# Context keys in four narrow pieces for two units, a fourth key buffer, and attention values one chunk at a time

## The chip, the cores and the metric

The kernel runs on one core of one Trainium2 chip. The metric is the device time of one execution in microseconds (us), lower is better. The kernel before takes 3268.74 us, the median of three runs (3264.41 to 3271.3). The core's engines are named as the profile names them: PE is TensorE's matrix multiply, PEld its weight load, DVE is VectorE, ACT is ScalarE, POOL is GpSimd, SP is SyncE, which here does nothing but issue DMAs. A "record" is one matmul instruction in the trace; a matmul on plain float32 operands leaves two, one on float32r operands leaves one.

## The reference

Two transformer layers over x of shape (4, 512, 320), with a context of shape (4, 1601, 192). All data are float32.

```python
def _attn(x, ctx, wq, wk, wv, wo, bo, heads):          # 20 heads of 16
    q = (x @ wq)...; k = (ctx @ wk)...; v = (ctx @ wv)...
    sim = jnp.einsum('bhid,bhjd->bhij', q, k) * scale
    a = jax.nn.softmax(sim, axis=-1)
    out = jnp.einsum('bhij,bhjd->bhid', a, v)
    return out @ wo + bo

for each of two layers:
    h1 = _ln(x, n1_g, n1_b)
    x = _attn(h1, h1, q1, k1, v1, o1_w, o1_b, 20) + x      # 512 keys
    h2 = _ln(x, n2_g, n2_b)
    x = _attn(h2, context, q2, k2, v2, o2_w, o2_b, 20) + x # 1601 keys
    h3 = _ln(x, n3_g, n3_b)
    a, g = jnp.split(h3 @ ff_w1 + ff_b1, 2, axis=-1)       # 1280 wide each
    x = (a * gelu(g)) @ ff_w2 + ff_b2 + x
```

## The kernel before

**Units.** Attention is cut into units: one batch element and four of the 20 heads. A layer has 20 self units (four batches of five groups `g`), then 20 cross units, then four feed-forward units, one per batch. `u.m` counts a unit within its kind and layer. A unit's keys come in chunks of 128: 4 in a self unit, 13 in a cross unit (the last has 65 keys). All 512 queries of the batch run beside one another as the moving columns.

**A unit's main loop** (`main`, L1098). A chunk is two rounds of two heads. For each head, two float32r matmuls give the scores (L1113: keys are held as a rounded high part and a low rest, and queries too), a third subtracts the row maximum (L1116, two rows of `units` by the row `m`), and ACT writes the exponential (L1126) to one of several places. These places are the tiles of `own` and some idle weight space (`places`, `place`). Beside each round's scores goes one piece of the next unit's row maxima: two heads, 128 queries and 512 keys (L926), reduced by DVE (L947). A self unit needs 8 such pieces, a cross unit 26. Exact maxima are so found one unit ahead, and `max_end` sends them by DMA to the row tile `m` (L1006).

After a chunk's scores come the values of earlier chunks (`values`, L1133, matmul L1141): the exponentials of a chunk are the moving operand and the value columns the weights. In a self unit one chunk at a time; in a cross unit two chunks at a time, added up in one PSUM bank. ACT copies the result (L1157) and POOL adds it to the unit's output `o` (L1158).

**Banks.** `ps_st` has four PSUM banks, taken in turn by score tiles, value tiles and projections; `ps_m` has two double banks, for maxima and for the middle two quarters of context keys and values.

**Projections.** A self unit's keys (`keys`, L749) and a unit's queries (`queries`, L717) are one bank each, or two for cross queries. A cross unit's keys (`keys_of_context`, L771): the context stands transposed in four quarters of 32 rows (`QT` = 384 keys each). For six blocks of 32 input features, four quarters and two halves of a quarter there is one matmul, 48 in all, of 32x64 weights by 224 keys (`HALF + 32`; L779). Two ACT copies and one DVE copy empty the banks into `kstage`, POOL splits high and low part (`split`, L624 and L625), and six DMAs (L796, L798) bring them to the key buffer, as rows of the unit's four heads. There are three key buffers `kbuf` in turn, four query buffers in turn, and a fifth query buffer for the first cross unit of a layer. That unit (`early`) is projected up to eight units ahead.

**What sets the order.** Everything beside the main loop waits in queues (`chains`), each entry with a cost, a due round and two conditions. A round counts half a chunk. After each chunk, `steps` runs the entries with the earliest due round, as far as a credit goes that `pace` earns from costs and due rounds. DMAs out of a staging tile go to the queue `slots`, at the earliest two rounds after their producer and at most four in a chunk (L391). `slots_soon` sets `kwhen` or `qwhen` after the last of them; a unit's maxima count as at hand three rounds later (`at_hand`). The function `giver` deals out the pieces of maxima: one a round, and more, in extra groups of two pieces, where a unit would otherwise not be done in time. If nothing is at hand and the next unit is near, `at_once` runs the projection and its DMAs on the spot.

**Values** of the keys (`add_values`): three blocks of four chunks and the tail of 65 keys, each for heads 0 to 7 (`i` = 0) and 8 to 19 (`i` = 1). L869 is the matmul of a block: 24 of 32x128 weights by 128 or 192 columns.

**Feed-forward** (`ff_main`): `gate` (L1267) keeps gelu outputs in three places of `own`.

## Time and profile before

| | |
|---|---|
| median of three runs | 3268.74 us (3264.41 to 3271.3) |
| profiled execution, own time | 3267.39 us |
| its span | 3265.6 us |
| mean granted PE clock | 0.967 |
| PE busy | 3117.7 us, 95% |
| DVE, ACT, POOL busy | 64%, 57%, 30% |

| stretch of the span, us | what runs | PE busy, us | granted clock |
|---|---|---|---|
| 0 to 452 | start, 20 self units of layer 0 | 396.2 | 0.91 |
| 452 to 1305 | most of its cross units | 828.1 | 0.98 |
| 1375 to 1625 | most of its feed-forward | 249.1 | 1.00 |
| 1690 to 2083 | self units of layer 1 | 355.9 | 0.87 to 1.00 |
| 2083 to 2950 | most of its cross units | 849.2 | 0.98 |
| 2950 to 3266 | the last unit, feed-forward | 311.0 | 1.00 |

The span runs from the first to the last instruction; the device time is 1.8 us more. A group line of the profile reads: line, engine, operation, written tile <- read tile with shape, count; then busy time and mean duration; then the engine's idle time just ahead and who ended most of it. A wait line reads: engine, line, awaited engine and line, us in total, times, the longest. A timeline line reads: start, duration, engine, line, operation, count, and in brackets the idle time ahead of it. The granted clock is 1 at full speed; the record of it shows only 1.0 and 0.5 in any moment, so 0.967 means 6.6% of the span at half clock. Durations of PE are modelled at their ends, so the times that count for it are those from start to start.

### The profile page before, as it was taken

To read this page: it belongs to the slowest core of one execution; us is meant where nothing else is said; L and a number is where in the kernel's file an instruction comes from. 1 tells how busy PE (TensorE), PEld (TensorE's weight loads), DVE (VectorE), ACT (ScalarE), POOL (GpSimd) and SP (SyncE) were. 2 spreads that over 40 slices of the span, in tenths; PEclk is the share of its full clock that TensorE was granted. 3 is DMA by queue.
4 is the path that set the end of the run, shared out by engine and by line. 5 is a ranking of instruction groups with operands and counts; after the bars stand their busy time and mean duration, and the time that the engine had idled before them with its cause. 6 is when DMAs were issued, how large, how long until landed. Compare 5 with 4: busy or idle time off the path is not lost.

```text
span 3265.6 us, 89144 instructions
## 1 busy us (share of the span) xinstructions
PE 3117.7 (95%) x36690; PEld 1686.7 (52%) x36690; DVE 2077.9 (64%) x2833; ACT 1866.6 (57%) x3721; POOL 972.6 (30%) x1141
## 2 busy tenths in 40 slices
PE   7899899999999999999998998999999999999999
PEld 3455455555455555455444554555555555554555
DVE  6766777777777776522246777777777777774221
ACT  3666566776667676711126665667767777765110
POOL 2435232323323332111114453324233333322000
PEclk8999899999999999999989998999999999999999
DMA  3433222211212211200113332212112111112000
GB/s 92 91 65 77 44 43 45 54 39 38 65 33 42 60 35 28 80 4 6 27 23 73 72 62 44 41 40 51 33 39 55 36 41 39 39 22 65 9 10 15
DMA packets 213039, 145.08 MB, mean 44 GB/s; under 512 B 65556, under 2 KB 203160, under 8 KB 212632
## 3 DMA queue, kind: packets, MB, share of 16 engines
q1 hardware_dynamic: 211368, 138.32, 19.1%
q8 instruction: 289, 4.73, 0.6%
q10 hardware_dynamic: 1264, 1.06, 0.1%
q14 instruction: 118, 0.97, 0.1%
HBM read 33.04 MB, written 7.93 MB: 13 GB/s over the span
## 4 chain that ended last, share of the span: by engine, by line
PE 80%; DVE 8%; ACT 4%; issue 3%; DMA 2%; SPq 2%; POOL 1%; ACTq 0%; DVEq 0%; POOLq 0%
PE av L1141 19%; PE st L1113 19%; PE fps L1246 9%; PE st L1116 6%; PE yps L1302 5%; PE sps L926 5%; DVE pm L947 3%; PE kps L779 3%; PE qps L717 3%; PE vps L869 3%; PE ops L1050 3%; DVE nmax L947 2%; PE fps L1259 2%; ACT pr L1126 2%; PE kps L749 1%
## 5 line engine op out<-in xcount | busy, mean ns | idle before, releaser
L947 DVE TENSOR_REDUCE pm<-sps 128x2 f32<-128x1024 f32 (+1 forms) x980 | 1127.6, 1195 | 225.3 <-PE sps L926 199.6
L1113 PE MATMUL st<-q,kT 32*128 32x512 f32 (+1 forms) x5440 | 1089.3, 445 | 40.5 <-DVE x L1057 8.0
L1126 ACT ACTIVATE pr<-st 128x512 f32<-128x512 f32 (+1 forms) x1791 | 947.1, 602 | 269.9 <-PE st L1116 252.1
L926 PE MATMUL sps<-kT,q 32*128 32x512 f32 (+1 forms) x6400 | 993.6, 411 | 52.9 <-DMA kT<-stage 20.1
L1113 PEld LDWEIGHTS st<-q,kT 32*128 32x128 f32 (+1 forms) x5440 | 537.6, 182 | 482.3 <-ACT pr L1126 160.2
L1116 PE MATMUL st<-m,units 2*128 2x512 f32 (+1 forms) x2720 | 655.3, 400 | 5.9 <-issue 2.1
L1141 PE MATMUL av<-pr,vals 128*32 128x512 f32 (+1 forms) x3582 | 644.5, 636 | 16.9 <-ACT pr L1126 10.3
L1158 POOL TENSOR_TENSOR o<-o,pr 128x512 f32<-128x512 f32 x236 | 302.2, 1281 | 951.2 <-ACT pr L1157 931.2
L926 PEld LDWEIGHTS sps<-kT,q 32*128 32x128 f32 x6400 | 474.1, 188 | 103.6 <-DVE pm L947 33.3
L947 DVE TENSOR_REDUCE nmax<-sps 128x2 f32<-128x1024 f32 (+1 forms) x356 | 381.2, 1109 | 175.2 <-PE sps L926 121.6
L1126 ACT ACTIVATE wself<-st 128x512 f32<-128x512 f32 (+1 forms) x801 | 427.6, 602 | 75.1 <-PE st L1116 68.6
L1116 PEld LDWEIGHTS st<-m,units 2*128 2x128 f32 (+1 forms) x2720 | 350.7, 184 | 42.8 <-issue 7.7
L1141 PE MATMUL av<-wself,vals 128*32 128x512 f32 (+1 forms) x1602 | 344.5, 635 | 3.6 <-ACT pr L1126 3.0
L1246 PE MATMUL fps<-hT,w 128*128 128x512 f32 x640 | 285.4, 599 | 1.8 <-DVE pr L1272 0.9
L1269 ACT ACTIVATE pr<-fps,b 128x512 f32<-128x512 f32 x80 | 50.6, 683 | 370.4 <-PE fps L1259 268.1
L1141 PEld LDWEIGHTS av<-pr,vals 128*32 128x32 f32 (+1 forms) x3582 | 114.3, 112 | 236.9 <-issue 101.4
L1158 POOL TENSOR_TENSOR o<-o,wself 128x512 f32<-128x512 f32 x89 | 114.0, 1281 | 381.5 <-ACT wself L1157 381.5
L1157 ACT COPY pr<-av 128x512 f32<-128x512 f32 x236 | 140.9, 597 | 135.7 <-PE av L1141 134.7
L1246 PEld LDWEIGHTS fps<-hT,w 128*128 128x128 f32 x640 | 118.9, 190 | 151.8 <-issue 146.6
L624 POOL TENSOR_SCALAR stage<-stage 128x256 fp32r<-128x256 f32 (+1 forms) x155 | 107.1, 691 | 218.6 <-ACT stage L725 135.5
L624 POOL TENSOR_SCALAR w<-w 128x896 fp32r<-128x896 f32 x40 | 98.1, 2452 | 147.0 <-DVE w L789 118.5
L1050 PE MATMUL ops<-wo,aT 112*32 112x160 f32 (+1 forms) x3072 | 128.5, 303 | 4.1 <-ACT pr L1126 2.8
(100 smaller groups left out, 3020.8 us busy)
## 6 DMA issues: line engine op xcount, KB each, us to landing
kT<-w SPq DMA_DIRECT2D x160, 192.0 KB
q<-stage SPq DMA_DIRECT2D x320, 64.0 KB
q<-stage SPq DMA_DIRECT2D x154, 128.0 KB
aT<-o SPq DMA_DIRECT2D x320, 32.0 KB
m<-turned SPq DMA_DIRECT2D x636, 2.0 KB
kT<-stage SPq DMA_DIRECT2D x156, 64.0 KB
w<-in_L_xattn_ff_w_dram SPq DMA_DIRECT2D x20, 256.0 KB
ctxT<-ctxT SPq DMA_DIRECT2D x24, 208.0 KB
```

The costliest lines, as they stand in the source:

```text
L624: eng.tensor_scalar(high.bitcast(F32R), x, 1.0, None, ALU.mult)
L926: nc.tensor.matmul(out, lhsT=u.q[rows, e, queries].bitcast(F32R), rhs=u.kT[rows, keys].bitcast(F32R), start=(e == 0), stop=(e == 1),)
L947: nc.vector.tensor_reduce(to[:, j : j + n], part, AX.X, ALU.max, negate=(ns == 1))
L1050: nc.tensor.matmul(ps[f : f + m, : D // 2], lhsT=aT[:n, k, t * P + f : t * P + f + m], rhs=wo[:n, k, cols], start=(k == 0), stop=(k == 2),)
L1113: nc.tensor.matmul(st[:r, :], lhsT=keys, rhs=u.q[rows, e, :].bitcast(F32R), start=(e == 0), stop=False)
L1116: nc.tensor.matmul(st[:r, :], lhsT=units_of[two_rows, :r].bitcast(F32R), rhs=u.mrow[two_rows, :].bitcast(F32R), start=False, stop=True,)
L1126: nc.scalar.activation(p[:r], st[:r], AF.Exp)
L1141: nc.tensor.matmul(ps[j * SLOT : (j + 1) * SLOT, :], lhsT=columns_of[:r, head : head + SLOT], rhs=pr.pop((c, j))[:r, :], start=(c == cs[0] ...
L1157: nc.scalar.copy(vo, ps)
L1158: nc.gpsimd.tensor_tensor(u.o, u.o, vo, ALU.add)
L1246: nc.tensor.matmul(ps, lhsT=w1[:, k, i * FF + c * P : i * FF + (c + 1) * P], rhs=u.hT[:, k, :], start=ahead and k == 0, stop=not ahead and ...
L1302: nc.tensor.matmul(ps[:, :D], lhsT=hid[c][:, t * P : (t + 1) * P], rhs=w2[:, c, :], start=(c == 0), stop=(c == NHC - 1),)
```

## The change

**Context keys in pieces.** `HALF` goes and `PIECE` = 104 comes. Two neighbouring units of one batch (g = 0 and 1, or 2 and 3) are projected together: weights of 128 columns for both units, four pieces of 104 keys of each quarter, 24 matmuls a piece. The units with g = 4, and the first two cross units of a layer, are still projected alone, in two pieces of 48 matmuls with 64 weight columns. Each piece has its own entry in the queue, cost 1.1 instead of 2.45, `apart` rounds from the next. `kstage` becomes two pairs of narrower tiles, so that a piece can be staged while the last one's DMAs wait. DMAs rise from 12 to 20 for a pair and from 6 to 10 for a unit alone.

**Buffers.** `kbuf` has four tiles instead of three. The fifth query buffer goes, and the first cross unit takes its turn among the four; its queries wait until the unit four places before is scored, and are due two units ahead. `own` has seven places instead of eight, and `gate` two of them for gelu outputs instead of three.

**Due rounds.** A self unit's projections are due ten rounds ahead of the unit before, not six. The context is due earlier by the pieces' distance. The second part of the values (`i` = 1) is due 12 rounds and more sooner.

**Values.** `values(c)` takes one chunk, in cross units too.

**`giver`.** Whether to run a projection on the spot is decided by the start of the unit whose maxima are missing, not by that of the next unit.

```diff
-HALF = QT // 2
+PIECE = (QT + 32) // 4
...
-    kbuf = [const.tile([P, 4 * QT + P], F32, name=f"kT{i}") for i in range(3)]
-    qbuf = [const.tile([P, 2, N], F32, name=f"q{i}") for i in range(5)]
+    kbuf = [const.tile([P, 4 * QT + P], F32, name=f"kT{i}") for i in range(4)]
+    qbuf = [const.tile([P, 2, N], F32, name=f"q{i}") for i in range(4)]
...
-    kw = 4 * (HALF + 32)
-    kstage = [w2_flat[:, 3 * D + i * kw : 3 * D + (i + 1) * kw].rearrange("p (a w) -> p a w", a=4) for i in range(2)]
-
-    own = const.tile([P, 8, N], F32, name="pr")
-    mine = [own[:, i, :] for i in range(8)]
+    kw = 4 * PIECE
+    kstage = [
+        [w2_flat[:, 3 * D + i * kw : 3 * D + (i + 1) * kw].rearrange("p (a w) -> p a w", a=4) for i in (j, j + 1)]
+        for j in (0, 2)
+    ]
+    own = const.tile([P, 7, N], F32, name="pr")
+    mine = [own[:, i, :] for i in range(7)]
...
         if u.cross:
-            u.kT, u.k0 = kbuf[(u.m + 1) % 3], 0
-            u.other = attn[i - 3] if u.m > 1 else attn[i - 6] if u.m else None
+            u.kT, u.k0 = kbuf[(1, 2, 0, 3)[u.m % 4]], 0
+            u.other = attn[i - (6 if u.m == 1 else 3 if u.m == 2 else 4)] if u.m else None
...
             u.other = attn[i - 3] if u.m == B * G - 1 else attn[i - 4] if u.m > 3 or u.m == 3 and u.l else None
-        u.qbuf = qbuf[4 if u.early else i % 4]
+        u.qbuf = qbuf[i % 4]
...
     def stages(kind="stage"):
-        empty(kind, kind == "stage")
+        empty(kind, 1)
         if kind == "kstage":
-            return [*kstage, None]
+            kstage.reverse()
+            return kstage[0]
...
-        due = lead(u) - 6
-        keys_due = due - 10 if u.cross else due
+        due = lead(u) - (6 if u.cross else 10)
+
+        keys_due, apart = (
+            (units[u.i - 4].start, 8) if u.early else (lead(u) - 5, 3) if u.m == 1 else (due - 10, 4)
+        ) if u.cross else (due, 0)
...
             if u.cross and not u.early:
-                add_context(u.l, u.b, lambda s: u.own.update(kv=s["cT"], tail=s["tail"]), keys_due - 2, free)
+                add_context(u.l, u.b, lambda s: u.own.update(kv=s["cT"], tail=s["tail"]), keys_due - 3 * apart - 2, free)
...
-        def keys_of_context():
+        mates = [v for v in units[u.i : u.i + 2] if v.cross and v.b == u.b]
+        alone = u.m < 2 or u.g == G - 1
+        mates = [u] if alone else mates if u.g % 2 == 0 else []
+        pieces = (
+            [[(u, h * 2 * PIECE + i * PIECE, h * GD) for h in range(2)] for i in range(2)]
+            if alone else [[(v, i * PIECE, e * GD) for e, v in enumerate(mates)] for i in range(4)]
+        )
+
+        def keys_of_context(i):
...
                     rows = slice(a * SLOT, (a + 1) * SLOT)
-                    for i in range(2):
-                        w = HALF + 32
+                    for v, at, to in pieces[i] if alone else pieces[i][:1]:
+                        n = GD if alone else 2 * GD
                         nc.tensor.matmul(
-                            ps[i * GD : (i + 1) * GD, :w],
-                            lhsT=wk_q[rows, k, u.g * GD : (u.g + 1) * GD],
-                            rhs=first.kvT[rows, k, i * HALF : i * HALF + w],
+                            ps[to : to + n, :PIECE],
+                            lhsT=wk_q[rows, k, u.g * GD : u.g * GD + n],
+                            rhs=first.kvT[rows, k, at : at + PIECE],
...
                         )
-            high, low, _ = stages("kstage")
-            for i, ps in enumerate(singles):
-                nc.scalar.copy(low[:, 3 * i, :], ps[:, : HALF + 32])
-            nc.vector.tensor_copy(low[:, 1:3, :], both[:, :, : HALF + 32])
+            high, low = stages("kstage")
+            for e, ps in enumerate(singles):
+                nc.scalar.copy(low[:, 3 * e, :], ps[:, :PIECE])
+            nc.vector.tensor_copy(low[:, 1:3, :], both[:, :, :PIECE])
             split(low, high)
-            def move(e, i):
-                to = rows_of(u.kT, e)
-                if i < 2:
-                    full = to[:, : 4 * QT].rearrange("d (a w) -> d a w", a=4)
-                    dma(out=full[:, :, i * HALF : (i + 1) * HALF], in_=(high, low)[e][i * GD : (i + 1) * GD, :, :HALF])
+            def move(e, v, at, where, tail):
+                to = rows_of(v.kT, e)
+                part = (high, low)[e][where : where + GD]
+                if tail:
+                    dma(out=to[:, 4 * QT :].rearrange("d (a w) -> d a w", a=4), in_=part[:, :, QT - at :])
                     return
-                dma(out=to[:, 4 * QT :].rearrange("d (a w) -> d a w", a=4), in_=(high, low)[e][GD:, :, HALF:])
-                if e:
-                    first.made["k"] += 1
-
-            slots_soon(u, [lambda e=e, i=i: move(e, i) for e in range(2) for i in range(3)], "kwhen", "kstage")
-            u.keyed = True
-            first.made["kv"] += 1
+                full = to[:, : 4 * QT].rearrange("d (a w) -> d a w", a=4)
+                w = min(PIECE, QT - at)
+                dma(out=full[:, :, at : at + w], in_=part[:, :, :w])
+
+            fs = [
+                lambda e=e, piece=piece, tail=tail: move(e, *piece, tail)
+                for piece in pieces[i] for e in range(2) for tail in range(1 + (piece[1] + PIECE > QT))
+            ]
+            last = i + 1 == len(pieces)
+            if last:
+                fs.append(lambda: first.made.update(kv=first.made["kv"] + len(mates)))
+                for v in mates:
+                    v.keyed = True
+            slots_soon(mates, fs, "kwhen" if last else "kpart", "kstage")
         def unread():
-            return u.n < 4 or u.early or attn[u.n - 4].early or attn[u.n - 4].scored == attn[u.n - 4].nch
+            return u.n < 4 or attn[u.n - 4].scored == attn[u.n - 4].nch
         def free():
-            return u.other is None or u.other.scored == u.other.nch
+            return all(v.other is None or v.other.scored == v.other.nch for v in mates or [u])
...
             for part in range(parts):
-                add(chain, (0.05 + 0.427 / parts,) * 3, lambda part=part: queries(part), due - 2, unread)
+                add(chain, (0.05 + 0.427 / parts,) * 3, lambda part=part: queries(part), units[u.i - 2].start if u.early else due - 2, unread)
...
         else:
-            add(chain, 2.45, keys_of_context, keys_due, free)
+            for i in range(len(pieces) if mates else 0):
+                after = (3 - i) * apart if len(pieces) == 4 else (1 - i) * 2 * apart
+                add(chain, 1.1, lambda i=i: keys_of_context(i), keys_due - after, free)
...
                     "values", 0.2 + w / 100, lambda i=i, s=s: values_of_context(i, s),
-                    units[u.i + g].start + 8 * s, lambda s=s, free=free: free(4 * s + 3),
+                    units[u.i + g].start + (4 * s - 12 if i else 8 * s), lambda s=s, free=free: free(4 * s + 3),
...
         last = nxt is None or nxt.kind == "ff"
-        def values(cs):
+        def values(c):
             if u.g in (0, 2):
-                until(lambda: units[u.i - u.g].vmade[u.g // 2] > cs[-1], "values")
+                until(lambda: units[u.i - u.g].vmade[u.g // 2] > c, "values")
             ps = ps_st.tile([P, N], F32, tag="st", name="av")
-            for c in cs:
-                r = min(P, u.nkeys - c * P)
-                for j in range(HG):
-                    head = (c * H + u.g * HG + j) * VW
-                    nc.tensor.matmul(
-                        ps[j * SLOT : (j + 1) * SLOT, :],
-                        lhsT=columns_of[:r, head : head + SLOT],
-                        rhs=pr.pop((c, j))[:r, :],
-                        start=(c == cs[0]),
-                        stop=(c == cs[-1]),
-                    )
-            u.valued = cs[-1] + 1
-
-            if cs[0] == 0:
+            r = min(P, u.nkeys - c * P)
+            for j in range(HG):
+                head = (c * H + u.g * HG + j) * VW
+                nc.tensor.matmul(
+                    ps[j * SLOT : (j + 1) * SLOT, :],
+                    lhsT=columns_of[:r, head : head + SLOT],
+                    rhs=pr.pop((c, j))[:r, :],
+                    start=True,
+                    stop=True,
+                )
+            u.valued = c + 1
+
+            if c == 0:
...
                 add_finish(u)
-        n = 2 if u.cross else 1
-        together = {min(c + n, u.nch) - 1: list(range(c, min(c + n, u.nch))) for c in range(0, u.nch, n)}
...
             flush()
-            if c in together:
-                late.append(lambda cs=together[c]: values(cs))
+            late.append(lambda c=c: values(c))
...
         def gate(c, pss):
-            gl = mine[5 + c % 3]
+            gl = mine[5 + c % 2]
...
                 hand = [v for v in ahead if left(v) and all(v.pairs) and at_hand(v)]
-                if not hand and ahead[0].start - 4 - clock["round"] > 1:
+                v = hand[0] if hand else next(v for v in ahead if left(v))
+                if not hand and v.start - 4 - clock["round"] > 1:
                     break
-                v = hand[0] if hand else next(v for v in ahead if left(v))
```

Each piece, projection and DMA group is entered for both units of a pair (`slots_soon` takes a list of units), and the context is held two rounds ahead of the first piece.

More of the change, by code (lines that the diff above doesn't have):

```diff
@@ L115 @@
     nc.gpsimd.memset(units_of, 1.0)
-    fill = qbuf[4][:, 0, :]
+    fill = qbuf[3][:, 0, :]
     nc.vector.memset(fill, 1.0)
@@ L640, in stages, with slots_soon @@
     def stages(kind="stage"):
-        empty(kind, kind == "stage")
+        empty(kind, 1)
         if kind == "kstage":
-            return [*kstage, None]
+            kstage.reverse()
+            return kstage[0]
         t = two.tile([P, 2, N // 2], F32, tag="stage", name="stage")
         return [t[:, e] for e in range(2)] + [t]
-    def slots_soon(u, fs, name, kind="stage"):
+    def slots_soon(us, fs, name, kind="stage"):
         fs = list(fs)
@@ L653, in last @@
             done()
-            setattr(u, name, -9 if start["on"] else clock["round"])
+            for u in us:
+                setattr(u, name, -9 if start["on"] else clock["round"])
         group = deque(fs + [last])
         groups[kind].append(group)
-        u.slots.append(group)
+        for u in us:
+            u.slots.append(group)
         if start["on"]:
@@ L704, in add_proj @@
             if u.cross:
-                add(chain, 0.0, hold_context, keys_due - 2, yes, lambda: "kv" in u.own)
+                add(chain, 0.0, hold_context, keys_due - 3 * apart - 2, yes, lambda: "kv" in u.own)
             else:
@@ L735, in queries @@
             slots_soon(
-                u, [lambda s=s, i=i: move(s, i) for i in range(2) for s in range(2)],
+                [u], [lambda s=s, i=i: move(s, i) for i in range(2) for s in range(2)],
                 "qwhen" if part == parts - 1 else "qpart",
@@ L765, in move @@
                 )
-            slots_soon(u, [lambda e=e, i=i: move(e, i) for e in range(2) for i in range(2)], "kwhen")
+            slots_soon([u], [lambda e=e, i=i: move(e, i) for e in range(2) for i in range(2)], "kwhen")
             u.keyed = True
             first.made["k"] += 1
-        def keys_of_context():
+        mates = [v for v in units[u.i : u.i + 2] if v.cross and v.b == u.b]
[6 more added lines that the diff above has]
+        def keys_of_context(i):
             pss, singles, both = quarter_banks("kps")
```

## The prediction

> **What bounds the kernel now.** I read the page's busy line and chain first, to see which engine sets the end; then the stages, to see where that engine loses time; then the timeline inside one context unit, to see what the changed lines do there. All rows are of the one profiled execution of the kernel before.
>
> ```profile
> PE 3117.7 (95%) x36690; PEld 1686.7 (52%) x36690; DVE 2077.9 (64%) x2833; ACT 1866.6 (57%) x3721; POOL 972.6 (30%) x1141
> PE 80%; DVE 8%; ACT 4%; issue 3%; DMA 2%; SPq 2%; POOL 1%; ACTq 0%; DVEq 0%; POOLq 0%
> L1158 POOL TENSOR_TENSOR o<-o,pr 128x512 f32<-128x512 f32 x236 | 302.2, 1281 | 951.2 <-ACT pr L1157 931.2
> L624 POOL TENSOR_SCALAR w<-w 128x896 fp32r<-128x896 f32 x40 | 98.1, 2452 | 147.0 <-DVE w L789 118.5
> ```
>
> TensorE is the bound: 95% busy and 80% of the chain. A step counts here if it changes TensorE's work, its waits or its clock; GpSimd at 30% has room. By stage (stretch in us, then its length, busy time and count of PE, PEld, DVE, ACT, POOL, granted clock, DMA share, GB/s):
>
> ```profile
> 452.00:1305.00 853.00, 828.10 (x11542) 462.69 (x11541) 631.55 (x774) 595.48 (x1199) 272.77 (x267) 0.98 0.20 44
> 1690.00:1790.00 100.00, 86.36 (x968) 41.94 (x962) 63.14 (x90) 60.25 (x121) 38.51 (x41) 0.90 0.34 73
> 1790.00:1975.00 185.00, 174.65 (x2598) 97.83 (x2598) 138.54 (x209) 119.45 (x245) 91.64 (x122) 1.00 0.30 64
> 1975.00:2083.00 108.00, 94.86 (x1234) 51.24 (x1234) 81.78 (x113) 57.64 (x118) 32.49 (x31) 0.87 0.21 42
> 2083.00:2950.00 867.00, 849.21 (x11854) 473.35 (x11855) 652.42 (x766) 620.07 (x1244) 279.46 (x272) 0.98 0.18 39
> ```
>
> The two cross stages (first and last line) take over half the time with TensorE 97% busy. The starts and ends of the self stages (second and fourth) lose more per us, to idle time and to a granted clock of 0.90 and 0.87. Busy hides slow work, so the timeline of two chunks in the middle of a cross unit, in which no other work falls until the values:
>
> ```profile
> 650.41 0.50 PE L1113 MATMUL st<-q,kT 32*128 32x512 f32 x2
> ...
> 652.12 0.18 PEld L1113 LDWEIGHTS st<-q,kT 32*128 32x128 f32 x1 [0.46 <-ACT wself L1126]
> ...
> 652.44 3.12 ACT L1126 ACTIVATE pr<-st 128x512 f32<-128x512 f32 x6
> ...
> 654.16 0.39 PE L1116 MATMUL st<-m,units 2*128 2x512 f32 x1
> ...
> 656.34 0.50 PE L1113 MATMUL st<-q,kT 32*128 32x512 f32 x2
> ```
>
> The first chunk takes 1.71 us (650.41 to 652.12), less than its four exponentials (4 x 0.52, from 3.12 us for six). So in the second chunk TensorE waits for a bank before nearly every score (652.12 on): 2.36 us of scores. The values of two chunks then take 2.18 us (654.16 to 656.34). The pair: 5.93 us. Where values follow every chunk, as already in self units and in the last chunk of a cross unit:
>
> ```profile
> 448.71 0.48 PE L1113 MATMUL st<-q,kT 32*128 32x512 f32 x2
> ...
> 450.38 0.62 PE L1141 MATMUL av<-w1r,vals 128*32 128x512 f32 x1
> ...
> 451.38 0.49 PE L1113 MATMUL st<-q,kT 32*128 32x512 f32 x2
> ```
>
> Here one chunk with its values takes 2.67 us; the median of 32 such bare chunks of self units is 2.73.
>
> **The change part by part.**
>
> **Values one chunk at a time: -50 us.** Each cross unit has 13 value groups instead of 7, so 240 more in 40 units. By work alone that loses: two single groups make a pair of chunks 2 x 2.73 = 5.46 us; a pair with no ACT wait is 1.71 + 3.59 = 5.30; +0.16 x 240 = +38 us. But pairs don't run at 5.30. Of 219 pairs in the two cross stages (452 to 1290, 2083 to 2945), the 89 at full clock whose first chunk has no side work take 5.89 us on average; 113 with side work there take 5.65 once that work is taken off at its price beside single values (query part 0.66, projection 0.82: both use the value matmuls' 128-row, 32-column tiles, and now always find one beside them). 17 more ran partly at half clock. So the gain at 2.73 a chunk is (89 + 17) x 0.43 + 113 x 0.19 = 67 us. I keep 50, since 0.035 us of new wait in each of 480 chunks is easily lost: ACT then has five passes of 0.52 us = 2.6 in 2.73. Bounds: -67, and +38 if every removed wait comes back. I lean to the gain because the 23 bare single-value chunks inside the cross stages also average 2.73. The 240 more copies (0.59 us, ACT) and adds (240 x 1.28 = 307 us, POOL) are hidden: POOL goes to some 39%. If POOL were late, banks would not be (the copy frees them), only the split of keys and the end of a unit.
>
> The Trainium skill, TensorEngine Tiling (Array Packing), Key Properties, speaks against this part: changing the tiling mode drains the array. The trace agrees that it costs: 0.32 us from the last score's start to the first value matmul's, 0.53 from the last value matmul's to the next score's. By that rule alone this part is the +38 us.
>
> **Half clock in cross: -22 us.** The clock record has 17 stretches at half clock there, 68 us in all, so at most 34 us lost. Every pair that they touch, 17, has a bare first chunk, so is one of those that wait for ACT; the self stretch with single values from 1790 to 1975 has none. Bounds: -39 (the 17 pairs take 8.16 us: 17 x 2.27 over their 5.89), and +15 if the extra switches leave the array as idle. I take a little over half.
>
> **Context keys: +12 us.** L779 runs 96 records (each matmul is two) in 12 groups of eight tiles, a group every 0.19 to 0.21 us for 224 columns; with its switches a unit costs TensorE 2.75 to 2.89 us. A pair of units now takes four pieces of 48 records of 32x128 weights by 104 columns. The nearest row is L869: 48 such records add 1.65 us at 128 columns and 2.09 at 192, so 1.49 at 104 on their line, 1.65 if the weight loads set it. Per pair 5.9 to 6.6 against 5.7: +3 to +13 us for 14 pairs. The 12 units done alone run two pieces of 96 records: the group's step falls to about 0.094 us, so 12 x 0.094 + 0.55 = 1.68 each, 3.35 against 2.85: +6. If these were bound per record as now (2.85 each), +34. Below: -5, if narrow pieces lose their switches beside values. I take +12. Two ACT copies and a DVE copy per piece (about 0.25 and 0.37 us by the rows of 128 and 256 columns) and the split (two passes of 1.1 us at most instead of 2.45 and 2.11) lie beside TensorE. DMAs on SP rise from 12 to 20 for a pair and 6 to 10 alone, 160 x 0.6 us = 96 us over the span, beside other work; DMA is 20% busy. SP stands for POOL's split of a unit's keys 342 us in 40 waits, 8.6 each, and behind it stand the next unit's row maxima and queries; a split of half the length shortens each wait, and there are twice as many.
>
> The Trainium skill, TensorE: Matmul & The Clock Gate, section on 56 against 53.3 ns, has a floor of some 25 ns between starts; by it the 192 records alone cost 4.8 us and the change +38 us. The trace's eight starts of one L779 group lie within 50 ns, so I go by the group's step.
>
> **Self keys due 4 rounds sooner, no forced projection while a unit is far off: -12 us.**
>
> ```profile
> PE sps L926 <- DMA kT<-stage: 20.1, 9, 5.7
> ```
>
> These nine waits are maxima whose keys were projected and moved at the last moment; all fall in the first half of self stages, before half-clock stretches. I take 12 of the 20 and nothing for the clock. Bounds: 0 (the first units cannot start earlier, and norms gate each batch) and -40 with the clock. The moved block is 24 records, an ACT copy, two POOL passes and four DMAs, now ahead of its unit's queries on POOL and SP, which have over four rounds to spare.
>
> **First cross unit of a layer: 0.** It loses its own query buffer: its queries now wait for the fourth unit before to be scored, so its 26 maxima fall in about 14 rounds instead of some 40. Before, they already come as 14 and 11 extra groups late in the self stage, with 42 and 30 us over the single-chunk price (stretches 290 to 452, 1975 to 2083). After, about 13 extra groups of 2.6 us of DVE (0.68 x 2 + 1.22) come in a burst: 24 to 43 us. Even; bounds -25 and +45 for both layers.
>
> **Fourth key buffer, values due sooner, seven places, two gelu buffers: 0.** Three buffers let a unit's keys start when the unit two before begins; four let a pair's start just then. The later values move 12 rounds and more ahead (48 records, two ACT copies and a DVE copy a block, no DMA); their work is the same, and weight loads wait 1.9 us in all behind a values copy. FF's ACT and DVE run far below TensorE (99.6% busy there). Bounds 0 and +60: see the second rival.
>
> Sum: -50 - 22 + 12 - 12 = -72. The profiled execution took 3267.4 us, 1.8 over its span, 1.3 under the median of the three times: 3195.
>
> **The rivals.**
> *ACT paces the single chunks.* For it: 2.6 of 2.73 us of ACT and any key or query copy on top; four banks now serve five tiles a chunk. Against: the single-value chunks already seen. Then values cost +38 and the clock stays: 3267 + 38 + 12 - 12 = 3305. It decides from 2.9 us a bare chunk: 480 x 0.15 = 72 us takes the whole gain. This one ends slower.
> *Keys late at a change of batch.* A pair's four pieces need the next batch's context, which waits for the tail values of the batch before (due as before, 24 rounds into its third unit), and SP is given four queued DMAs a chunk, 20 for a pair. If half of 26 maxima come as extra groups, six changes x 6.5 groups x 3 us (the half-clock price above) = 117: 3312. Against: about 20 rounds are there for it.
> *The burst at the first cross unit costs its upper bound*, 45 us: 3240.
> *Narrow pieces change nothing and all half-clock loss goes too*: 3267 - 67 - 39 - 20 = 3141.
>
> **How the numbers follow.** My forecast 0.44 (own range 3165 to 3230), ACT 0.22, late keys 0.11, burst 0.13, all gains 0.10. The ACT case reaches from 3245 to 3305, so a few parts of it are no change. From 3140 to 3300 some 2 in 10 are left out. 0.2% is 6.5 us, about what this measurement can tell from no change. Faster: 0.44 + 0.10 + 0.11 of burst + 0.02 of ACT = 0.67; same 0.06; slower 0.27.
>
> **What would show it.** Bare cross chunks at 2.7 us with no ACT wait before a score; a granted clock of 0.99 or more in cross; key pieces at 1.5 to 1.7 us; the wait for kT below 10 us; POOL near 39%. Wrong if bare chunks take 2.9 or more, if extra groups of maxima appear at batch changes, or if the end of the self stages falls under a clock of 0.85.

## The result: 52 us less, and where it came from

The changed kernel takes **3214.66 us** (median of 4, 3211.83 to 3218.06) against 3266.57 (3262.43 to 3271.3) for the kernel before in the same comparison: ratio **0.9841, 95% interval 0.9823 to 0.9859**. The profiled execution took 3214.11, its span is 3212.3. The forecast was 3195, so the direction held and 20 of 72 us are missing.

The page of the changed kernel: busy line, chain by engine, GpSimd's adds, and the row of the score matmuls with the idle time before them at its end.

```profile
PE 3036.1 (95%) x37842; PEld 1644.5 (51%) x37842; DVE 2093.8 (65%) x2869; ACT 1963.7 (61%) x4029; POOL 1267.8 (39%) x1449
PE 77%; DVE 6%; ACT 6%; SPq 4%; DMA 3%; issue 2%; POOL 1%; ACTq 0%; POOLq 0%; DVEq 0%
L1144 PE MATMUL st<-q,kT 32*128 32x512 f32 (+1 forms) x5440 | 1001.0, 443 | 44.5 <-ACT w L810 26.8
L1188 POOL TENSOR_TENSOR o<-o,pr 128x512 f32<-128x512 f32 x359 | 461.2, 1285 | 750.4 <-ACT pr L1187 728.1
```

TensorE has 82 us less of busy time although it runs 1152 more instructions. GpSimd went from 30% to 39%, as forecast, and its adds still wait for ACT (728 us), not ACT for them. One row is new: scores that wait 26.8 us behind line 810, the ACT copy of projected context keys into their stage. It carries the rest of this text.

For the comparison I cut both spans at the same events: the moments when the row maxima of given units are finished. Rows by stage (stretch in us, length, then busy and count of PE, PEld, DVE, ACT and POOL, granted clock, DMA share, GB/s). Before: middle of the first self stage (units 5 to 15), then the two cross stages up to their last unit.

```profile
130.80:333.90 203.10, 184.98 (x2621) 102.70 (x2618) 141.60 (x231) 121.94 (x252) 90.33 (x121) 0.96 0.34 75
495.60:1339.10 843.50, 820.23 (x11169) 453.44 (x11166) 627.10 (x766) 592.25 (x1189) 265.69 (x261) 0.97 0.19 43
2124.80:2947.90 823.10, 806.76 (x11168) 448.17 (x11168) 619.46 (x721) 591.64 (x1187) 266.66 (x261) 0.98 0.18 39
```

After, the same three:

```profile
130.20:312.80 182.60, 169.98 (x2663) 95.92 (x2667) 139.22 (x228) 121.06 (x251) 92.52 (x125) 0.97 0.36 80
476.80:1313.60 836.80, 794.41 (x11466) 435.97 (x11463) 637.68 (x775) 638.38 (x1327) 401.07 (x399) 0.96 0.19 42
2082.70:2894.90 812.20, 779.22 (x11460) 430.83 (x11457) 623.90 (x734) 637.25 (x1324) 400.85 (x399) 0.98 0.18 39
```

In cross, TensorE's busy time fell by 26 and 28 us, but the stages got only 7 and 11 us shorter, and the clock did not rise. The whole sum, with the experiments' profiled spans beside it (us; in brackets the time at half clock in the cross stages):

| stretch | before | after | values singly, alone | self rounds, alone | third stage pair |
|---|---|---|---|---|---|
| self, start to unit 15, both layers | 617.5 | 585.8 | 616.2 | 599.6 | 593.6 |
| units 15 to 21, into cross | 321.9 | 326.9 | 314.6 | 314.0 | 321.5 |
| cross with its last unit | 1749.9 (82) | 1724.3 (92) | 1711.0 (68) | 1752.0 (82) | 1680.5 (37) |
| FF, both layers | 576.4 | 575.3 | 578.0 | 573.5 | 575.3 |
| span | 3265.6 | 3212.3 | 3219.8 | 3239.0 | 3171.0 |

So 32 us came from the self stages (forecast 12), 26 from cross (forecast 60), 5 were lost between them (forecast 0).

A bare chunk of a cross unit after the change, from one first score (620.46) to the next (623.17):

```profile
620.46 0.50 PE L1144 MATMUL st<-q,kT 32*128 32x512 f32 x2
...
621.52 2.07 ACT L1157 ACTIVATE wself<-st 128x512 f32<-128x512 f32 x4 [0.66 <-PE st L1147]
...
622.18 1.06 PE L1171 MATMUL av<-pr,vals 128*32 128x512 f32 x8 [0.29 <-ACT wself L1157]
...
623.17 0.44 PE L1144 MATMUL st<-q,kT 32*65 32x512 f32 x2
```

It takes 2.71 us (the median of such chunks is 2.72); the four exponentials (2.07 us) now stand idle 0.66 us before the scores are there. No score matmul shows a wait; only the values wait 0.29 us for the last exponential. That is the forecast mechanism. TensorE's longest waits over the whole span (us in total, times, longest) are others:

```profile
PE av L1171 <- ACT pr L1157: 40.7, 170, 0.3
PE st L1144 <- ACT w L810: 26.8, 15, 3.0
PE st L1147 <- DMA m<-turned: 23.3, 19, 4.1
...
PE sps L957 <- DMA kT<-stage: 8.4, 5, 3.9
```

The wait for self keys fell from 20.1 to 8.4 us. The second and third row are new (the row maxima `m` cost 1.7 us before). What is behind the second shows at a change of batch; ACT, PE, and the DMA queue of SP, each line with its idle time and what ended it in brackets:

```profile
579.73 6.16 SPq L822 DMA_DIRECT2D kT<-w  x8
...
581.61 2.94 PE L801 MATMUL kps<-ctxT,w 32*128 32x104 f32 x96
...
584.98 0.61 ACT L810 COPY w<-kps 128x104 f32<-128x104 f32 x2 [2.47 <-DMA kT<-w]
...
585.28 0.86 PE L1144 MATMUL st<-q,kT 32*128 32x512 f32 x2 [0.72 <-ACT w L810]
...
587.11 2.26 SPq L822 DMA_DIRECT2D kT<-w  x3
587.93 0.39 ACT L810 COPY w<-kps 128x104 f32<-128x104 f32 x2 [2.35 <-DMA kT<-w]
...
588.23 0.94 PE L1144 MATMUL st<-q,kT 32*128 32x512 f32 x2 [1.61 <-ACT w L810]
```

Here all four pieces of a pair are overdue, because they waited for the new batch's context, and two go into one chunk (96 records at 581.61). There are two pairs of stage tiles, so the third and the fourth piece must wait until the DMAs of the first and second have left them. SP sends these eight DMAs in 6.16 us, 0.77 each. The copy into the stage stands in ACT's queue until then (2.47 and 2.35 us), the chunk's exponentials stand behind it, and TensorE finds no free bank for scores: the keys' results hold theirs until the copy has read them.

### The profile page after: what moved, and what is told of

Read it like the earlier page. It is cut to its first block, busy times and chain, and to the rows that moved or that the text cites. A ratio compares the mean times of both kernels' runs of the same rounds, so it can differ in the third digit from the quotient of the medians.

```text
span 3212.3 us, 92658 instructions
## 1 busy us (share of the span) xinstructions
PE 3036.1 (95%) x37842; PEld 1644.5 (51%) x37842; DVE 2093.8 (65%) x2869; ACT 1963.7 (61%) x4029; POOL 1267.8 (39%) x1449
## 4 chain that ended last, share of the span: by engine, by line
PE 77%; DVE 6%; ACT 6%; SPq 4%; DMA 3%; issue 2%; POOL 1%; ACTq 0%; POOLq 0%; DVEq 0%
PE av L1171 19%; PE st L1144 16%; PE fps L1271 9%; PE st L1147 6%; PE yps L1327 5%; PE sps L957 4%; ACT pr L1157 3%; PE ops L1081 3%; PE qps L726 3%; PE kps L801 3%; PE vps L900 3%; DVE pm L978 2%; SPq L1037 2%; PE fps L1284 2%; DVE nmax L978 2%
## 5 line engine op out<-in xcount | busy, mean ns | idle before, releaser
L1157 ACT ACTIVATE pr<-st 128x512 f32<-128x512 f32 (+1 forms) x1710 | 906.7, 602 | 259.7 <-PE st L1147 250.6
L1144 PE MATMUL st<-q,kT 32*128 32x512 f32 (+1 forms) x5440 | 1001.0, 443 | 44.5 <-ACT w L810 26.8
L957 PE MATMUL sps<-kT,q 32*128 32x512 f32 (+1 forms) x6400 | 989.2, 410 | 31.2 <-DVE pm L978 11.3
L1188 POOL TENSOR_TENSOR o<-o,pr 128x512 f32<-128x512 f32 x359 | 461.2, 1285 | 750.4 <-ACT pr L1187 728.1
L1144 PEld LDWEIGHTS st<-q,kT 32*128 32x128 f32 (+1 forms) x5440 | 504.6, 184 | 471.3 <-ACT pr L1157 149.7
L1147 PE MATMUL st<-m,units 2*128 2x512 f32 (+1 forms) x2720 | 614.2, 402 | 24.4 <-DMA m<-turned 23.3
L1157 ACT ACTIVATE wself<-st 128x512 f32<-128x512 f32 (+1 forms) x867 | 462.9, 603 | 103.2 <-PE st L1147 101.6
L1188 POOL TENSOR_TENSOR o<-o,wself 128x512 f32<-128x512 f32 x191 | 245.2, 1284 | 342.1 <-ACT wself L1187 339.9
L1147 PEld LDWEIGHTS st<-m,units 2*128 2x128 f32 (+1 forms) x2720 | 313.4, 185 | 70.8 <-issue 30.9
L1187 ACT COPY pr<-av 128x512 f32<-128x512 f32 x359 | 217.1, 605 | 25.8 <-PE av L1171 24.2
L801 PEld LDWEIGHTS kps<-ctxT,w 32*128 32x128 f32 (+1 forms) x4992 | 115.4, 164 | 53.8 <-ACT pr L1157 28.7
```

Source lines behind the costliest of these rows:

```text
L801: nc.tensor.matmul(ps[to : to + n, :PIECE], lhsT=wk_q[rows, k, u.g * GD : u.g * GD + n], rhs=first.kvT[rows, k, at : at + PIECE], start=(k ...
L957: nc.tensor.matmul(out, lhsT=u.q[rows, e, queries].bitcast(F32R), rhs=u.kT[rows, keys].bitcast(F32R), start=(e == 0), stop=(e == 1),)
L1144: nc.tensor.matmul(st[:r, :], lhsT=keys, rhs=u.q[rows, e, :].bitcast(F32R), start=(e == 0), stop=False)
L1147: nc.tensor.matmul(st[:r, :], lhsT=units_of[two_rows, :r].bitcast(F32R), rhs=u.mrow[two_rows, :].bitcast(F32R), start=False, stop=True,)
L1157: nc.scalar.activation(p[:r], st[:r], AF.Exp)
L1187: nc.scalar.copy(vo, ps)
```

## The experiments

The theory after the first comparison: the values and the self rounds each bring a gain by themselves, and the reuse of the two stage pairs gives part of it back in cross, by the wait and by the half clock that follows it. Each run has a kernel before measured beside it (medians 3271.25 to 3274.32 us), and its ratio is to that. The rivals: the parts were worth less than forecast in the first place; the narrow pieces themselves are what costs (more records, more copies, more DMAs); or the late maxima rows are.

**1. Values one chunk at a time, in the kernel before.**

```diff
-        n = 2 if u.cross else 1
+        n = 1
```

> The kernel before with one thing of the change: values one chunk at a time in cross units. My theory (waits for ACT in pairs of chunks were what the cross stages lost, and key pieces and late row maxima gave back a part of it in the changed kernel): about 3210 us, cross stages 45 to 60 us shorter together, bare cross chunks at 2.8 us, less than 35 us at half clock in cross. Rival (the split values are worth little, the gain came from the self stages): 3245 us or more. Rival (the extra switches of the array cost their work): 3290 to 3305 us.

Measured: 3225.4 us, ratio 0.987 (0.9845 to 0.9895), span 3219.8: **43 us less** by the ratio, 46 by the span, 39 of them in cross. That is between my 3210 and the rival's 3245. The ACT rival is out. The two cross stages with their last units still take 1711 us, and the half clock only went from 82 to 68 us: the pairs that waited for ACT are gone here, and the slow stretches are not. So the reason I had given for the half clock fell with this run. The first cross stage:

```profile
493.80:1320.40 826.60, 791.23 (x11182) 427.05 (x11182) 635.27 (x766) 634.94 (x1298) 403.32 (x369) 0.98 0.20 44
```

It is 10 us shorter than the changed kernel's (836.80), which has the same values and less than 300 records more; the second is 3 us shorter (809.50 against 812.20). Whatever else the change did in cross, it cost.

**2. Self projections due ten rounds ahead, in the kernel before.**

```diff
-        due = lead(u) - 6
+        due = lead(u) - (6 if u.cross else 10)
```

> The kernel before with one thing of the change: self projections due ten rounds ahead instead of six. My theory now (the units' maxima are then at hand when their rounds begin, so the extra groups of maxima and the half clock after them go from the self stages): 3235 to 3245 us, all of it in the self stages. As forecast at first, for the waits on keys alone: 3255 us. Rival (it was the rule on running projections on the spot): 3267 us.

Measured: 3242.86, ratio 0.9917 (0.9901 to 0.9933): **27 us less**. That is the range I had given. Nearly all of it lies in units 5 to 15 of the first layer and in the step into cross:

```profile
133.90:316.50 182.60, 167.82 (x2546) 93.75 (x2540) 142.20 (x229) 120.85 (x250) 93.45 (x125) 0.99 0.37 81
```

That is 20.5 us less than before's 203.10, and TensorE is busy 17 us less: before, 7 groups of maxima in this stretch stood in an extra place of their own instead of beside a chunk, because their keys were not there; now one does. The clock went from 0.96 to 0.99. In the second layer the groups fall from 5.5 to 1 too, but the stretch keeps its length (195.2 against 194.1), since 20 us of it instead of 7 run at half clock.

**3. The `giver` rule, in the kernel before.**

```diff
-                if not hand and ahead[0].start - 4 - clock["round"] > 1:
-                    break
                 v = hand[0] if hand else next(v for v in ahead if left(v))
+                if not hand and v.start - 4 - clock["round"] > 1:
+                    break
```

> The kernel before with one thing of the change: whether a projection is run on the spot is decided by the start of the unit whose maxima are missing. My theory: 3260 to 3267 us. Rival (this rule gave the self stages' gain): 3240 us.

Measured: 3281.26 (3262.47 to 3284.75, 10 executions), ratio 1.0031 (1.002 to 1.0042). Nothing gained, 0.3% lost if anything, where I had expected 3260 to 3267; its profiled execution has a span of 3260.7, so a single profile would have said the opposite. The gain in the self stages is the earlier round's.

**4. These three together, in the kernel before.** (The three edits above.)

> The kernel before with single-chunk values, earlier self projections and the rule on running projections together, and none of the pieces, the shared query buffer or the fourth key buffer. My theory (the gains add, and the key pieces are a small loss): 3175 to 3190 us, faster than the changed kernel. Rival (the pieces and the fourth buffer bring some of the changed kernel's gain): 3220 us or more.

Measured: 3199.03, ratio 0.9787 (0.9766 to 0.9808), span 3198.8, 70 us less. The gains add (43 + 27), the time is 9 us above my range, and this kernel is **faster than the changed one by half a per cent**. The rest of the change, keys in pieces and buffers, costs some 15 us as it stands.

**5. The earlier self round taken out of the changed kernel.**

```diff
-        due = lead(u) - (6 if u.cross else 10)
+        due = lead(u) - 6
```

> The changed kernel with self projections due six rounds ahead again. My theory (the earlier due round alone makes the self stages' gain): 3235 to 3245 us, extra groups of maxima back in the self stages. Rival (the later projection of the first cross unit makes it too): 3220 us or less.

Measured: 3241.37, ratio 0.9896 (0.9875 to 0.9917), span 25 us over the changed kernel's. The stretch from unit 5 to 15 goes back to:

```profile
134.60:339.90 205.30, 182.58 (x2694) 101.30 (x2694) 142.20 (x228) 122.76 (x253) 93.98 (x127) 0.94 0.33 74
```

and 4.5 extra groups come back in each layer. Taken out here, the part is worth 25 us by the spans and 18 by the ratios, against 27 put in alone.

**6. Whole-unit keys in the changed kernel.** Projection, stage, DMAs and due rounds of the context keys as before; four key buffers, four query buffers, seven places and all other rounds as changed. Of the edit, the entry in the queue:

```diff
...
-            for i in range(len(pieces) if mates else 0):
-                after = (3 - i) * apart if len(pieces) == 4 else (1 - i) * 2 * apart
-                add(chain, 1.1, lambda i=i: keys_of_context(i), keys_due - after, free)
+            add(chain, 2.45, keys_of_context, keys_due, free)
...
```

> The changed kernel with context keys of a whole unit at once, as before (48 matmuls of 224 columns, one stage, their old due round), but its four key and four query buffers, seven places and all due rounds of self keys and values. My theory (the pieces cost about 15 us, the rest of the buffers nothing): 3197 to 3204 us. Rival (the loss against the three parts alone comes from the shared query buffer and the late first cross unit): 3212 us or more.

Measured: 3192.35 (3184.03 to 3194.22), ratio 0.975 (0.9732 to 0.9768), span 3182.2. **The pieces cost 30 us** as the change has them (span 3212.3), twice what I had expected. Against run 4 the span is 17 us shorter (12 by the ratios, whose intervals just touch), which is what the fourth key buffer, the later values' rounds, the seven places, the two gelu buffers and the early queries bring together; they were not tried one by one. The cross stages:

```profile
471.60:1295.00 823.40, 783.31 (x11182) 421.16 (x11186) 640.80 (x764) 635.14 (x1298) 403.86 (x369) 0.98 0.20 44
2058.80:2864.80 806.00, 776.12 (x11176) 418.06 (x11176) 627.86 (x720) 634.36 (x1295) 403.40 (x369) 0.99 0.18 40
```

This run alone does not say whether the narrow matmuls cost or their stage.

**7. The pieces kept at least four rounds apart,** so that two never fall into one chunk.

```diff
-                add(chain, 1.1, lambda i=i: keys_of_context(i), keys_due - after, free)
+                add(chain, 1.1, lambda i=i: keys_of_context(i), keys_due - after, free, lambda: clock["round"] >= clock.get("piece", -9) + 4)
```

(`clock["piece"]` is set to the current round at the start of each piece.)

> The changed kernel, but a piece of context keys is entered at the earliest four rounds (two chunks) after the last one, so that its stage has been sent off. My theory (27 us of score waits behind key copies, which stand behind the DMA out of a reused stage, and the half clock after them): those waits below 8 us, the cross stages 12 to 25 us shorter together, 3192 to 3203 us. Rival (the pieces then come too late for the next unit's maxima, extra groups appear at changes of batch): 3220 us or more.

Measured: 3251.04, ratio 0.993 (0.9911 to 0.995), span 37 us over the changed kernel's. TensorE's waits:

```profile
PE av L1172 <- ACT pr L1158: 38.0, 157, 0.5
PE st L1145 <- ACT stage L734: 35.3, 13, 4.6
PE st L1148 <- DMA m<-turned: 21.3, 19, 2.4
```

No wait for the key copy is left, but the keys are now late at the changes of batch: 8 groups of maxima stand alone in each cross stage (0 in the changed kernel), and the scores wait 35.3 us behind copies of queries. The rival's case came. The four pieces have no time to lose there; the next run gives them room in place of distance.

**8. A third pair of stage tiles** for the context keys, in weights that are idle while cross units run; nothing else changed. It is taken into the turn at the third cross unit of a layer and out of it at the first of the next.

```diff
+    third = [t.rearrange("p (a w) -> p a w", a=4) for t in (w2_flat[:, 3 * D + 4 * kw : 3 * D + 5 * kw], w1r[:, 4 * CTX : 4 * CTX + kw])]
...
-        empty(kind, 1)
+        empty(kind, len(kstage) - 1 if kind == "kstage" else 1)
         if kind == "kstage":
-            kstage.reverse()
-            return kstage[0]
+            kstage.append(kstage.pop(0))
+            return kstage[-1]
...
+            if i == 0 and u.m == 0 and len(kstage) > 2:
+                kstage.pop(next(n for n, t in enumerate(kstage) if t is third))
+            if i == 0 and u.m == 2:
+                kstage.append(third)
```

> The changed kernel with a third pair of key stages (in idle weight space, from the third cross unit on), so that the third piece of a burst need not wait for the first one's DMA; nothing else moves. My theory (a reused stage is what the key copies on ACT wait for): score waits behind key copies fall from 27 to below 10 us, 10 to 20 us less at half clock in cross, 3195 to 3205 us. Rival (the pieces cost through the number of their copies, DMAs and matmuls, not through the stage): 3210 to 3218 us with the waits gone or not.

Measured: **3171.21 (3164.43 to 3176.43), ratio 0.9684 (0.9659 to 0.9709)**, span 3171.0: the fastest of all, 41 us under the changed kernel by the spans and 24 below the range I had given. TensorE's waits in its first cross stage:

```profile
PE av L1176 <- ACT pr L1162: 10.4, 41, 0.3
PE av L1176 <- ACT wself L1162: 7.3, 29, 0.3
PE st L1152 <- DMA m<-turned: 5.2, 6, 1.7
PE sps L962 <- DVE pm L983: 4.3, 13, 1.5
PE st L1149 <- ACT w L815: 1.2, 1, 1.2
```

In the changed kernel the last of these stands first, with 15.1 us there and 7.3 in the second cross stage. ACT's idle time before the key copies themselves (us, times), in the changed kernel and then with the third pair:

```profile
  PE kps L801: 58.1, 62
  DMA kT<-w: 44.4, 15
```

```profile
  PE kps L802: 61.3, 71
  DMA kT<-w: 4.0, 2
...
  DMA kT<-w1r: 2.1, 1
```

And the two cross stages:

```profile
477.40:1289.60 812.20, 781.65 (x11466) 430.16 (x11463) 637.69 (x775) 638.23 (x1327) 400.52 (x399) 0.98 0.20 43
2060.20:2853.30 793.10, 767.78 (x11460) 425.21 (x11457) 622.79 (x734) 636.05 (x1323) 400.54 (x399) 1.00 0.19 40
```

The work is the same, record for record, and cross is 43.8 us shorter. That can be accounted for: 22.4 us of waits behind the key copy in cross became 1.9, so 20.5; and the half clock in cross went from 92 to 37 us, half of which is lost work, so at most 27.5. Sum 48, some of it counted twice, since a wait can lie at half clock. Of the 92 us, 41 are in the seven stretches (of 15) that begin during or just after a wait for a key copy; that the rest of the fall has the same cause is not shown. The main question is settled: the stage's reuse, not the narrow matmuls, gave the gain back. With it gone the pieces beat whole units (run 6) by 24 us in cross. The traces show where: in the two cross stages the waits for maxima rows fall from 16.8 to 9.1 us, those of maxima for DVE's reduction from 14.4 to 7.9, those for `vals` copies from 3.1 to below the rows shown, and the half clock from 51 to 37 us.

**9 and 10. The late maxima rows.** The wait for `m` (23.3 us, new) might come from other DMAs ahead of it in SP's queue. Run 9 takes run 4's kernel and keeps SP free of DMAs of projections (keys and queries) in the third chunk from the end of a unit, when `m` is about to be sent; the new last argument of `steps` is the most such DMAs that it may send there:

```diff
...
-            steps(None, 1 if extra or c == u.nch - 1 else 2)
+            steps(None, 1 if extra or c == u.nch - 1 else 2, 0 if c == u.nch - 3 and not last else 4)
```

> The three parts alone (single-chunk values, earlier self projections, the rule on running projections) and, new, no DMA of projections in the chunk after which the row maxima are sent. My theory (row maxima m come 24 us late in all because such DMAs stand before them on SP): waits for m below 8 us, 3175 to 3190 us. Rival (DVE, not SP, makes them late): waits as before, 3195 to 3205 us.

Measured: 3291.77, ratio 1.0051 (1.0035 to 1.0067), 93 us over run 4 and far above both ranges:

```profile
PE sps L926 <- DMA kT<-stage: 56.7, 16, 9.6
...
PE st L1116 <- DMA m<-turned: 20.3, 21, 1.8
```

The wait for `m` hardly moved (24.5 to 20.3), and self units, which have few chunks, got their keys late (56.7 us). Run 10 takes run 6's kernel and sends half of the `m` DMAs from GpSimd's queue:

```diff
-                queue = (nc.sync, nc.scalar)[e] if start["on"] else nc.sync
+                queue = (nc.sync, nc.scalar)[e] if start["on"] else (nc.sync, nc.gpsimd)[e]
```

> The changed kernel with whole key units (as in the run before) and the row maxima's eight DMAs shared by two queues, SP's and GpSimd's. My theory (eight issues of 0.5 us on one queue are what makes the rows late): waits of TensorE for m from 34 to below 15 us and less half clock, 3170 to 3185 us. Rival (they are late by DVE or by landing): waits of 25 us or more, 3188 to 3200 us.

Measured: 3193.58, ratio 0.9751 (0.973 to 0.9771): no difference from run 6's 0.975.

```profile
PE st L1123 <- DMA m<-turned: 19.9, 8, 3.8
...
PE st L1123 <- issue: 9.2, 7, 3.8
...
PE st L1123 <- DMA kT<-w: 5.4, 2, 3.4
```

The 33.9 us of run 6 are still there, as 34.5 under three names. But the run did not make the sending shorter where it is late. One such wait in run 6, from the finished maxima to the score that waits, and then one in run 10:

```profile
614.29 0.21 DVE L1007 STREAM_TRANSPOSE turned<-nm 128x32 f32<-128x32 f32 x1
614.57 4.62 SPq L1013 DMA_DIRECT2D m<-turned  x8
620.38 0.50 PE L1123 MATMUL st<-m,units 2*128 2x512 f32 x2 [1.18 <-DMA m<-turned]
```

```profile
606.99 0.21 DVE L1007 STREAM_TRANSPOSE turned<-nm 128x32 f32<-128x32 f32 x1
...
610.30 2.28 POOL L1013 DMA_DIRECT2D m<-turned  x4
...
614.95 0.79 PE L1123 MATMUL st<-m,units 2*128 2x512 f32 x2 [3.05 <-DMA m<-turned]
```

In run 6 SP begins at once, and the eight sends take 4.62 us of the 5.88 from the finished maxima to the score; the same holds for the other waits of over 0.5 us in its two cross stages. In run 10 GpSimd's four sends stand behind its split of keys and end later than SP's eight did. So run 10 does not decide against its theory: a shorter sending stays untested. In the changed kernel's cross stages, four of the seven such waits also have queries' DMAs ahead of the rows on SP, some 1.5 us. The single chunks bring a part of the wait in (run 1 alone has 14 us of it in cross), the earlier self rounds another (13.3 us in run 2); in the changed kernel 14.7 of the 23.3 us lie in the self stages.

## Why the prediction was right, and where it was not

The forecast of the sign and the range held, in part by luck: cross came 34 us short of its 60, and the self stages gave 20 more than their 12. Its terms, one by one:

- **Values, −50: right in kind, too high in size.** Alone −43 (run 1); of its 39 us in cross some 7 are half clock (82 to 68 us), so 32 stand against the 50. The bare chunk is at 2.72 as said (2.7), its mean 2.80 over the 179 in the two cross stages of the changed kernel that run wholly at full clock. The wait for the last exponential (55.6 us in 229 waits over the span) does not make it longer: the 81 chunks that have it take 2.71 in the median, the 98 without 2.80. What had no price are row maxima that come late: 14 us of waits in run 1's cross stages, where the kernel before had 1.7 in the whole span. The Trainium skill's rule that a change of the tiling mode drains the array (TensorEngine Tiling (Array Packing), Key Properties) was set against this part, with +38 as the estimate; run 1 decides against that sum, though not against the rule, since the switches are still in the 2.72.
- **Half clock in cross, −22: the step that failed, twice.** In the changed kernel the time at half clock rose from 82 to 92 us, so +5, and the clock in cross is 0.96 and 0.98 where 0.99 was asked for. Its reason was wrong too: that every pair they touch "is one of those that wait for ACT" is true of the trace of before and no cause, since run 1 has no such pairs and still 68 us. In the changed kernel 14 of the 15 slow stretches in cross begin during or within 7 us of a wait of TensorE of 0.8 to 3.1 us, seven of them at a key copy; with the key copies' waits gone (run 8) it is 37 us, a saving of 22.5 against before. So the size came out in another kernel and by another way, which is luck.
- **Context keys, +12: the matmuls were sized right, the stage was left out.** A piece for two units adds 1.35 us to a chunk, a piece for one 1.53 (said: 1.5 to 1.7), a whole unit 2.5 (said: 2.75 to 2.89), so that the difference holds though most prices were too high: 14 x (4 x 1.35 − 2 x 2.5) + 12 x (2 x 1.53 − 2.5) = +12. The Trainium skill's floor of some 25 ns between starts (TensorE: Matmul & The Clock Gate, section on 56 against 53.3 ns) would have given +38, by the prediction's estimate, and is not what this trace shows for eight small tiles side by side: their starts lie 6.7 ns apart. But "two ACT copies and a DVE copy per piece … lie beside TensorE" was false: with two stage pairs, ACT's copy waited for a DMA (44.4 us in 15 waits), and the exponentials behind it in ACT's queue waited with it. Against whole units the term came to +30 as built (run 6), and to −11 by the spans, −22 by the ratios, with a third pair (run 8). The cover for those copies was costed as if the stage were always free. The text even had what was needed: 20 DMAs for a pair, sent at 0.6 us each (0.77 here), against chunks into which two pieces can fall.
- **Self keys, −12: undersized.** The self stages gave −32 in place; alone the part gave −27, 18 of them in the self stages (run 2). I priced the nine waits for keys (20.1 us, now 8.4) and "nothing for the clock", and left out that maxima whose keys are late are also computed in extra groups of their own: 7 and 5.5 in units 5 to 15 before, none after. `giver`, which shared this term, is worth nothing (run 3).
- **First cross unit, 0: right within 5 us.** Units 15 to 21 got 2.3 and 2.7 us longer; the extra groups there went from 9.5 to 11 in each layer. The forecast had 14 and 11 groups before, in longer stretches, and a burst of some 13 after, and called it even.
- **Buffers, rounds and places, 0: −12 to −17 together** (run 6 against run 4), a small gain, if it is one, that no step had.

Of the rivals, *ACT paces the single chunks* is refuted by run 1, whose bare chunks take 2.76 us in the median; the rival's mark was 2.9. *Keys late at a change of batch* had the place half right: 11.3 of the 22.4 us of waits behind key copies in cross lie at the first pair of a new batch, the other 11.1 at the second pair of a batch, where pieces also come close together (why was not examined). Its form was another. It expected extra groups of maxima, which came only in run 7 (8 in each cross stage); in the changed kernel the planner gets the keys through in time, and pays by ACT's queue. *The burst* and *all gains* did not come. Of the signs listed, pieces for one unit (1.53; those for two were cheaper still, 1.35), the wait for kT (8.4), POOL (39%), the chunk and the absence of extra groups came; the clock did not.

## What to carry to other kernels

When a block is cut into smaller pieces, count the stage buffers and the transfers that must leave them, at the place where pieces come closest together and not on average. An in-order engine that copies into a reused stage takes everything queued behind it along: here 44 us of ACT waiting became 27 us of TensorE waiting, with 41 us at half clock beside it, and one more pair of tiles brought it back. And price work that comes late twice: by its wait, and by the extra place that its successors then take in the order.

## What the runs showed of the chip that I had not expected

- The time of a block of small matmuls went by its groups of tiles and their columns, not by its records: 96 records of 64 weight columns take 1.24 us from first to last start, 48 records of 128 weight columns 1.33, both 12 groups by 104 columns (0.11 to 0.12 us a group); at 224 columns a group takes 0.20. Within a group of eight the starts lie 6.7 ns apart.
- The clock falls to half, for 3.4 to 6.8 us, at TensorE waits of only 0.8 to 3.1 us in 14 of the 15 stretches in the changed kernel's cross stages; the 15th, of 10.2 us, has no gap above 0.3 us in the 7 us ahead. In the kernel before it does so in 17 stretches of the cross stages with no gap above 0.5 us in the 6.8 us ahead of them; what sets it off there stays open.
